# Adapter weights as the stationary operand of the setup's matmuls, and the first unit's step sizes on VectorE

## The chip, the cores and the metric

The kernel runs on one core of a Trainium2 chip. The core has five engines with queues of their own: TensorE (PE, with its weight loads listed apart as PEld), VectorE (DVE), ScalarE (ACT), GpSimd (POOL) and SyncE (SP), which here only issues DMAs. Each engine works its queue in the order of the program and waits on semaphores for the others. The metric is the device time of one execution in microseconds (us); less is better.

## What is computed

The reference runs four layers over x, 16 sequences of 256 steps and 256 features, all in float32, with a condition vector of 256 numbers for each sequence. Layer 0 makes adapter matrices from the condition and applies them:

```python
h = gelu(layernorm(ada_emb, ln_g, ln_b) @ W1 + b1)     # (16, 256)
w = h @ W2 + b2                                        # (16, 256 * 8 * 4)
a1, bb1, a2, bb2 = split(w, 4)                         # each (16, 256, 8): feature, rank
y = gelu((x @ a1) @ bb1.T)                             # per sequence
x = x + (y @ a2) @ bb2.T
```

Layer 1 is a selective state space model, forward and backward in time. Its step sizes are dt = softplus(xs @ xproj_w + bias); for each of 512 channels and 64 states the recurrence is h = h * exp(dt * A) + dt * xs * B, and the output sums h * C over the states. Layers 2 and 3 are attention and feed-forward blocks whose scales, shifts and gates are matmuls of the same condition ("modulation").

## The kernel before

**The loop.** There are 32 units: 16 sequences by two directions. For each unit the kernel takes 64 states one after another. GpSimd makes the products dt * xs * B (`drive`, L926), ScalarE the decays exp(dt * A) (`decay`, L941), VectorE scans over time (L969) and multiplies by C (L972; for three states of eight GpSimd does it, L976), and TensorE adds up over the states (L987). The next unit's front and the rest of a sequence's layers are interleaved by Python generators: `step(gen)` records the next piece of a generator, up to its next `yield`.

**The setup.** Ahead of the loop stands the setup, which this change is about.

- L169 to L191: SP issues the loads of the condition, of W1 (`w_ada`), of many small bias rows, and of the first tiles of W2. `load_w2(i)` loads the i-th of eight tiles of W2: 256 rows by 1024 columns in two halves `w` of 128 rows each, 512 KB. Columns are 128 features by 8 ranks with the rank running fastest. The halves take turns in the 11 buffers (`NH`) that later hold the loop's `h`. Three tiles are loaded up front (L194).
- L197 to L247: transposes, the layer norm and W1 give `hid`, the activated hidden layer, with features on the partitions: 2 halves of 128 x 16 sequences.
- L994 to L1037: the tile loop, which makes the four adapter matrices (`mats`: `lows[0]`, `turned[0]`, `lows[1]`, `turned[1]`, each of 2 halves of 128 features). For tile i, `hid` is the stationary operand (128 x 16) and the W2 tile streams past it, 512 columns at a time (L1005). The result has the 16 sequences on its partitions, so it is copied to SBUF (`wrow`, L1008, one half by VectorE and one by ScalarE), and one step later eight transposes of 16 x 128, one for each rank, turn it (L1020). VectorE adds the bias b2 (L1021). When both halves of a `turned` matrix are there, they are transposed once more (L1030) and written to scratch memory in DRAM (`spill`, L1035). The loop issues the load of tile i + 3, and at i = 2 that of the first sequence (`load_adapter(0)`) and of the first unit's projection weights (`load_front(0)`: `w_in`, `w_dt`). From i = 4 on it takes a step of the generator `modulation` (L215: 12 matmuls with 128 x 128 weights and 16 moving columns).
- L1038 `load_ups(0)`: the first sequence's rows of `spill` come back as `hi`.
- `front(0)` (L373): the adapter is applied (L341 `px` to L362), layer norm, input projection (L393, `w_in`), Silu (L399), the projections to B and C (L404) and to the step sizes (L423, `w_dt`). Softplus follows as max(p, 0) + log(1 + exp(-|p|)), with a correction for the rounding of 1 + exp(-|p|): ScalarE makes the pieces (L438 to L447) and GpSimd puts them together in four operations over 128 x 1024 elements (L452, L455, L458, and L461, which makes `dtx` = dt * xs, the input of every product in L926).
- Meanwhile the second unit's front and `late()` begin: `late()` makes the modulations of the later layers (L215 again, closed by L222 and L228 on VectorE), pads the weights of layer 3 (L1061 to L1086) and derives some biases (L1110).

**What sets the order.** Operations go to a scheduler, which may place them ahead of others in an engine's queue; those in `tc.keep_in_program_order` keep their place. Matmul results use PSUM tiles of 128 x 512 from a pool of two (`bank1`, `bank2`), so a third one waits until one of the two before it is read out. SP issues DMAs in the order of its queue: one that waits for a free buffer holds up those behind it.

Of the kernel before, what the change touches and what calls it, by code (L numbers as in the profile page):

```python
# [8 lines left out]
F32 = mybir.dt.float32  # L9
AF = mybir.ActivationFunctionType  # L10
ALU = mybir.AluOpType
# [4 lines left out]
P = 128  # L16
B, T, D = 16, 256, 256
DC = D // P
NT = T // P
RANK = 8  # L20
DI = 512
IC = DI // P
# [32 lines left out]
def kernel(ctx: ExitStack, tc: tile.TileContext, a: dict, out: bass.AP):  # L55
    nc = tc.nc
# [4 lines left out]
    ident = const.tile([P, P], F32, name="ident")  # L61
# [76 lines left out]
    def chunked(w):  # L138
        return w.rearrange("(c p) f -> p c f", p=P)

    def bank1(name="bank1"):
        return ps_g.tile([P, 512], F32, tag="bank2", name=name)
# [14 lines left out]
    def halves(t):  # L157
        return t.rearrange("p (c t) -> p c t", c=2)
# [6 lines left out]
    p2 = early.enter_context(tc.tile_pool(name="p2", bufs=2))  # L165
# [17 lines left out]
    b2 = p1.tile([P, 4, DC, RANK], F32, name="b2")  # L183
    nc.sync.dma_start(b2, a["L0_cond_b2"].rearrange("(m c p r) -> p m c r", m=4, c=DC, p=P))

    def load_w2(i):
        ws2 = []
        for k in range(DC):
            w = s3.tile([P, P * RANK], F32, tag="h", name="w2", bufs=NH)
            nc.sync.dma_start(w, a["L0_cond_W2"][k * P : (k + 1) * P, i * P * RANK : (i + 1) * P * RANK])  # L190
            ws2.append(w)  # L191
        return ws2

    w2s = [load_w2(i) for i in range(3)]  # L194

    pt = bank1("pt_rows")
    nc.tensor.transpose(pt[:, :P], rows, ident)  # L197
# [42 lines left out]
    hid = p1.tile([P, DC, B], F32, name="hid")  # L240
# [81 lines left out]
    def load_adapter(b):  # L322
        dtxs[2 * b] = s2.tile([P, IC, T], F32, name="dtx")
        xin = dtxs[2 * b][:, 0:2]
        nc.sync.dma_start(xin, a["x"][b].rearrange("(t p) d -> p t d", p=P))
        adapt[b] = xin
# [38 lines left out]
    def load_front(u):  # L365
        d = ("fwd", "bwd")[units[u][1]]
        wi = ws.tile([P, DC, 2 * DI], F32, tag="ws", name="w_in")
        nc.sync.dma_start(wi, chunked(a[f"L1_cond_{d}_in_w"]))
        wd = ws.tile([P, IC, DI], F32, tag="ws", name="w_dt")
        nc.sync.dma_start(wd, chunked(a[f"L1_cond_{d}_xproj_w"])[:, :, 0:DI])  # L370
        wfront[u] = (wi, wd)

    def front(u):  # L373

        b, d = units[u]
        name = ("fwd", "bwd")[d]
        if d == 0:
            yield from adapter(b)
            hT = s1.tile([P, DC, T], F32, name="hTm")
            sq = s1.tile([P, DC, T], F32, name="sqm", tag="uu")  # L380
            yield from layernorm(
                xs[b], hT, sq, bank1,
                lambda c: m_mamba[:, 2 + c, b : b + 1], lambda c: m_mamba[:, c, b : b + 1], T,
            )
            normed[b] = hT
        hT = normed[b]
        w_in, w_dt = wfront.pop(u)
        xz = s2.tile([P, 2 * IC, T], F32, name="xz")
        for m in range(0, 2 * IC, 2):
            px = halves(bank1("pxz"))  # L390
            for j in range(2):
                for c in range(DC):
                    nc.tensor.matmul(  # L393
                        px[:, j], w_in[:, c, (m + j) * P : (m + j + 1) * P], hT[:, c],
                        start=(c == 0), stop=(c == DC - 1),
                    )
                yield
            nc.scalar.copy(xz[:, m : m + 2], px)
        nc.scalar.activation(xz, xz, AF.Silu)  # L399
        exp_table()  # L400
        yield
        pb = bank1("pbc")
        for c in range(IC):
            nc.tensor.matmul(pb[:, :T], w_bc[d][:, c], xz[:, c], start=(c == 0), stop=(c == IC - 1))  # L404
        bc = s1.tile([P, T], F32, name="bc", tag="uu")
        nc.scalar.copy(bc, pb[:, :T])
        bd = bdram.tile([P, T], F32, name="bd")
        nc.sync.dma_start(bd, bc)
        yield
        pt = bank1("pct")  # L410
        for t in range(NT):
            nc.tensor.transpose(pt[:, t * P : (t + 1) * P], bc[:, t * P : (t + 1) * P], ident)
        cT = s2.tile([P, NT, NS], F32, name="cT")
        nc.scalar.copy(cT, pt[:, :T].rearrange("p (t s) -> p t s", t=NT)[:, :, NS:])
        yield


        pr = s1.tile([P, IC, T], F32, name="pr")
        for m in range(0, IC, 2):
            pp = halves(bank1("pdt"))  # L420
            for j in range(2):
                for c in range(IC):
                    nc.tensor.matmul(  # L423
                        pp[:, j], w_dt[:, c, (m + j) * P : (m + j + 1) * P], xz[:, c],
                        start=(c == 0), stop=(c == IC - 1),
                    )
                yield
            for j in range(2):
                nc.scalar.activation(  # L429
                    pr[:, m + j], pp[:, j], AF.Identity, bias=col(f"L1_cond_{name}_dt_bias", m + j)  # L430
                )
            yield
        if u + 1 < len(units):
            load_front(u + 1)
        if d == 1:
            dtxs[u] = s2.tile([P, IC, T], F32, name="dtx")
        dtx = e = dtxs.pop(u)
        nc.scalar.activation(e, pr, AF.Abs)  # L438
        yield
        nc.scalar.activation(e, e, AF.Exp, scale=-1.0)  # L440
        nc.scalar.activation(pr, pr, AF.Relu)
        yield
        dt = s2.tile([P, IC, T], F32, name="dt")
        uu = s1.tile([P, IC, T], F32, name="uu")
        nc.scalar.activation(uu, e, AF.Identity, bias=1.0)
        nc.scalar.activation(dt, uu, AF.Ln)
        nc.scalar.activation(uu, uu, AF.Identity, bias=minus)  # L447
        yield
        yield
        yield  # L450
        yield
        tc.keep_in_program_order(nc.gpsimd.tensor_tensor(uu, e, uu, ALU.subtract))  # L452
        yield
        yield
        tc.keep_in_program_order(nc.gpsimd.tensor_tensor(dt, dt, uu, ALU.add))  # L455
        yield
        yield
        tc.keep_in_program_order(nc.gpsimd.tensor_tensor(dt, dt, pr, ALU.add))  # L458
        yield
        yield  # L460
        tc.keep_in_program_order(nc.gpsimd.tensor_tensor(dtx, dt, xz[:, 0:IC], ALU.mult))  # L461
        st[u] = (xz, cT, bd, dt, dtx)
        yield

# [527 lines left out]

    turned = [p1.tile([P, DC, B, RANK], F32, name=f"up{k}") for k in range(2)]
    mats = [lows[0], turned[0], lows[1], turned[1]]
    wrows = {}
    for i in range(9):
        if i < 8:
            w2 = w2s[i]  # L1000
            wrow = p2.tile([B, P * RANK], F32, tag="wrow", name="wrow")
            for n in range(2):
                pw = bank1("pw")
                for k in range(DC):
                    nc.tensor.matmul(  # L1005
                        pw[:B], hid[:, k], w2[k][:, n * 512 : (n + 1) * 512], start=(k == 0), stop=(k == DC - 1)
                    )
                (nc.scalar.copy if n else nc.vector.tensor_copy)(wrow[:, n * 512 : (n + 1) * 512], pw[:B])  # L1008
            wrows[i] = wrow
            if i + 3 < 8:  # L1010
                w2s.append(load_w2(i + 3))
            if i == 2:
                load_adapter(0)
                load_front(0)
        if i > 0:
            m, c = (i - 1) // 2, (i - 1) % 2
            wv = wrows.pop(i - 1).rearrange("b (d r) -> b d r", r=RANK)
            pw = bank1("pwt")
            for r in range(RANK):
                nc.tensor.transpose(pw[:, r * B : (r + 1) * B], wv[:, :, r], ident[:B, :B])  # L1020
            nc.vector.tensor_tensor(  # L1021
                mats[m][:, c],
                pw[:, : RANK * B].rearrange("p (r b) -> p b r", b=B),
                b2[:, m, c, :].unsqueeze(1).to_broadcast([P, B, RANK]),
                ALU.add,
            )
            if m % 2 and c:
                ph = bank1("pmt")
                for c in range(DC):
                    nc.tensor.transpose(  # L1030
                        ph[:, c * P : (c + 1) * P], mats[m][:, c].rearrange("p b r -> p (b r)"), ident
                    )
                upT = p1.tile([P, D], F32, name=f"upT{m}")
                nc.scalar.copy(upT, ph[:, :D])
                nc.sync.dma_start(spill[:, m // 2], upT)  # L1035
        if i > 3:
            step(mamba)  # L1037
    load_ups(0)  # L1038
    drain(mamba)
# [99 lines left out]
    for k in range(len(steps) + BEHIND):  # L1139
        if k < len(steps):  # L1140
            u, s = steps[k]
# [11 lines left out]
        if k >= BEHIND:  # L1153
            u, s = steps[k - BEHIND]
            if s == NS - 1:
                b, d = units[u]
# [4 lines left out]
                for i in range(2):  # L1161
                    py = halves(bank1("py"))
                    for j in range(2):
                        c = 2 * i + j
# [45 lines left out]
```

## Time and profile before

| | |
|---|---|
| median of 3 runs | 7628.08 us (7628.05 to 7632.17) |
| the profiled execution | 7630.37 us, its span 7628.6 us |
| busy: TensorE, VectorE, ScalarE, GpSimd | 82%, 90%, 70%, 91% of the span |
| mean granted TensorE clock | 0.928 |
| tile loop: first matmul L1005 to last turn L1030 | 27.14 to 73.23 us |
| first product L926, first scan L969 | 135.09, 137.47 us |

The span runs from the first to the last recorded instruction. A share of busy time is a mean over stages that have different limits: setup, loop and tail are to be read apart. "Idle before" in a row names what ended an engine's wait. The granted clock is the share of its full clock that TensorE's throttle lets through.

### The profile page before, as it was taken

What the parts mean: (1) busy time and instruction counts of PE and PEld (TensorE: products, weight loads), DVE (VectorE), ACT (ScalarE), POOL (GpSimd) and SP (SyncE); (2) the same over time, 40 slices, a digit from 0 to 9 for tenths busy, and PEclk for the clock granted to TensorE, in tenths of its full rate; (3) what the DMA queues carried; (4) which work ended last, traced back from release to release, by engine and by line L of the source; (5) the groups of instructions that cost most, each with busy time, mean ns of one, the idle gap of its engine ahead of it and who ended that gap; (6) DMA issues with size and microseconds to landing.
All of it is one profiled execution on the core that took longest, in us unless ns stands there. A gap on an engine that the chain in (4) does not pass through costs nothing. (4 is left out here: it accounts for less than half of the span.)

```text
span 7628.6 us, 100211 instructions
## 1 busy us (share of the span) xinstructions
PE 6253.0 (82%) x35215; PEld 4947.6 (65%) x35215; DVE 6886.1 (90%) x6951; ACT 5370.7 (70%) x12013; POOL 6912.3 (91%) x2991
## 2 busy tenths in 40 slices
PE   6568888888888888888888888888888888888778
PEld 4456666666667666666666667666666666667655
DVE  3988998999999999999999999899999999999972
ACT  3567776777767777776777777777776777777653
POOL 3999999999999999999999999999999999999960
PEclk8679999999999999999999999999999999999999
DMA  4112232222322222232222222222232222222211
GB/s 167 52 60 93 85 103 73 92 90 87 108 79 96 79 95 94 92 103 73 85 100 86 100 86 97 78 92 93 87 105 78 92 85 96 94 92 92 72 64 49
DMA packets 331642, 675.87 MB, mean 89 GB/s; under 512 B 24724, under 2 KB 204032, under 8 KB 326784
## 3 DMA queue, kind: packets, MB, share of 16 engines
q1 hardware_dynamic: 331136, 669.44, 26.0%
q8 instruction: 278, 4.55, 0.2%
q14 instruction: 228, 1.87, 0.1%
HBM read 650.22 MB, written 10.75 MB: 87 GB/s over the span
## 5 line engine op out<-in xcount | busy, mean ns | idle before, releaser
L969 DVE TENSOR_TENSOR_SCAN h<-decay,h 128x512 f32<-128x512 f32 x4096 | 4735.2, 1204 | 271.5 <-ACT decay L941 189.3
L926 POOL TENSOR_TENSOR h<-dtx,bb 128x1024 f32<-128x1024 f32 x2048 | 4794.8, 2370 | 79.9 <-PE y L987 79.8
L987 PE MATMUL y<-ident,h 128*128 128x128 f32 x16384 | 2457.7, 296 | 836.8 <-POOL h L976 798.8
L987 PEld LDWEIGHTS y<-ident,h 128*128 128x128 f32 x16384 | 2083.4, 153 | 1216.4 <-POOL h L976 940.9
L941 ACT ACTIVATE decay<-dt,a_neg_bwd 128x255 f32<-128x255 f32 x4096 | 1814.5, 469 | 824.1 <-DVE h L969 777.0
L941 ACT ACTIVATE decay<-dt,a_neg_fwd 128x255 f32<-128x255 f32 x4096 | 1807.9, 471 | 641.1 <-DVE h L969 598.9
L976 POOL TENSOR_TENSOR h<-h,cb 128x1024 f32<-128x1024 f32 x768 | 1816.5, 2365 | 199.5 <-DVE h L969 172.0
L972 DVE TENSOR_TENSOR h<-h,cs 128x1024 f32<-128x1024 f32 x1280 | 1526.0, 1204 | 73.7 <-PE cs L956 62.9
L956 PE MATMUL cs<-ident,cT 128*128 128x128 f32 x2560 | 503.6, 290 | 88.5 <-DVE h L972 86.1
L956 PEld LDWEIGHTS cs<-ident,cT 128*128 128x128 f32 x2560 | 332.1, 146 | 163.4 <-DVE h L972 123.9
L573 PE MATMUL sc<-k,q 64*128 64x256 f32 x960 | 283.1, 417 | 17.7 <-ACT ex L582 17.0
L393 PE MATMUL pxz<-hTm,w_in 128*128 128x256 f32 x1024 | 275.8, 387 | 15.4 <-DVE maxima L683 12.3
L582 ACT ACTIVATE ex<-sc,nmax 128x256 f32<-128x256 f32 x480 | 222.1, 468 | 71.9 <-DVE nmax L578 69.1
L701 PE MATMUL scT<-qk,kd 128*128 128x256 f32 x984 | 248.8, 385 | 28.6 <-DVE qk L692 23.1
L680 PE MATMUL sc<-kd,qk 128*128 128x512 f32 x490 | 252.0, 621 | 14.2 <-DVE maxima L683 10.0
L596 ACT COPY exT<-pt 128x512 f32<-128x512 f32 x240 | 139.8, 583 | 162.7 <-PE pt L592 162.4
L423 PE MATMUL pdt<-xz,w_dt 128*128 128x256 f32 x1024 | 245.9, 383 | 0.0
L573 PEld LDWEIGHTS sc<-k,q 64*128 64x128 f32 x960 | 167.0, 193 | 99.8 <-ACT ex L582 32.9
L701 PEld LDWEIGHTS scT<-qk,kd 128*128 128x128 f32 x984 | 176.1, 190 | 58.3 <-ACT pr L429 24.9
L393 PEld LDWEIGHTS pxz<-hTm,w_in 128*128 128x128 f32 x1024 | 179.2, 193 | 43.2 <-DVE maxima L683 15.7
L423 PEld LDWEIGHTS pdt<-xz,w_dt 128*128 128x128 f32 x1024 | 189.4, 193 | 21.8
L578 DVE TENSOR_REDUCE nmax<-sc 128x2 f32<-128x512 f32 x240 | 162.1, 676 | 35.7 <-PE sc L573 35.5
(348 smaller groups left out, 7530.1 us busy)
## 6 DMA issues: line engine op xcount, KB each, us to landing
bb<-bd SPq DMA_DIRECT2D x512, 512.0 KB
cb<-bd SPq DMA_DIRECT2D x256, 384.0 KB
l2w<-in_L_cond_W_dram SPq DMA_DIRECT2D x32, 1024.0 KB
l3w<-in_L_cond_W_dram SPq DMA_DIRECT2D x32, 1024.0 KB
l1w<-in_L_cond_mlp_w_dram SPq DMA_DIRECT2D x48, 512.0 KB
w_in<-in_L_cond_fwd_in_w_dram SPq DMA_DIRECT2D x16, 1024.0 KB
w_dt<-_L_cond_fwd_xproj_w_dram SPq DMA_DIRECT2D x16, 1024.0 KB
w_in<-in_L_cond_bwd_in_w_dram SPq DMA_DIRECT2D x16, 1024.0 KB
```

What stands on the lines that cost most here:

```text
L393: nc.tensor.matmul(px[:, j], w_in[:, c, (m + j) * P : (m + j + 1) * P], hT[:, c], start=(c == 0), stop=(c == DC - 1),)
L423: nc.tensor.matmul(pp[:, j], w_dt[:, c, (m + j) * P : (m + j + 1) * P], xz[:, c], start=(c == 0), stop=(c == IC - 1),)
L573: nc.tensor.matmul(sc[:, t], q[base : base + 64, ch, t * P : (t + 1) * P], k[base : base + 64, ch], start=True, stop=True,)
L680: nc.tensor.matmul(sc, q[:, g, t * P : (t + 1) * P], kd[g % 2][:, 2 * i : 2 * i + 2], start=True, stop=True)
L701: nc.tensor.matmul(sc[:, kt], kd[g % 2][:, j, kt * P : (kt + 1) * P], q[:, g], start=True, stop=True)
L926: nc.gpsimd.tensor_tensor(h, st[u][4], bb.unsqueeze(1).to_broadcast([P, IC, T]), ALU.mult)
L941: nc.scalar.activation(dc[:, j, 1:T], st[u][3][:, c, when], AF.Exp, scale=a_neg[d][:, c, s : s + 1])
L956: nc.tensor.transpose(cs[:, i % 2, t * P : (t + 1) * P], st[u][1][:, t, s : s + 1].to_broadcast([P, P]), ident)
L969: nc.vector.tensor_tensor_scan(hv, dv, hv, 0.0, ALU.mult, ALU.add)
L972: nc.vector.tensor_tensor(h, h, c.unsqueeze(1).to_broadcast([P, IC, T]), ALU.mult)
L976: nc.gpsimd.tensor_tensor(h, h, c.unsqueeze(1).to_broadcast([P, IC, T]), ALU.mult)
L987: nc.tensor.matmul(ys[u][:, t, c * P : (c + 1) * P], h[:, c, t * P : (t + 1) * P], ident, start=(s == 0 and c == 0), stop=(s == NS - 1 and ...
```

## The change

In the tile loop the operands change places. For each rank the 128 features of a W2 half are the stationary operand, every eighth of its columns (`w2[k][:, :, r]`), and `hid` (16 columns) moves; two halves add up in PSUM, and the result has the features on its partitions at once. The `wrow` copies and the transposes L1020 go, and the bias is added straight from the matmul's PSUM tile. A tile has 16 matmuls of 16 moving columns where it had 4 of 512 and 8 transposes. Five tiles are loaded up front instead of three, and the modulation's steps begin one tile earlier in the count (`i > 2`). Lastly, the four step size operations go to VectorE for unit 0 alone.

```diff
-    w2s = [load_w2(i) for i in range(3)]
+    w2s = [load_w2(i) for i in range(5)]
...
+        pool = nc.gpsimd if u else nc.vector
...
-        tc.keep_in_program_order(nc.gpsimd.tensor_tensor(uu, e, uu, ALU.subtract))
+        tc.keep_in_program_order(pool.tensor_tensor(uu, e, uu, ALU.subtract))
...
-        tc.keep_in_program_order(nc.gpsimd.tensor_tensor(dt, dt, uu, ALU.add))
+        tc.keep_in_program_order(pool.tensor_tensor(dt, dt, uu, ALU.add))
...
-        tc.keep_in_program_order(nc.gpsimd.tensor_tensor(dt, dt, pr, ALU.add))
+        tc.keep_in_program_order(pool.tensor_tensor(dt, dt, pr, ALU.add))
...
-        tc.keep_in_program_order(nc.gpsimd.tensor_tensor(dtx, dt, xz[:, 0:IC], ALU.mult))
+        tc.keep_in_program_order(pool.tensor_tensor(dtx, dt, xz[:, 0:IC], ALU.mult))
...
-    for i in range(9):
-        if i < 8:
-            w2 = w2s[i]
-            wrow = p2.tile([B, P * RANK], F32, tag="wrow", name="wrow")
-            for n in range(2):
-                pw = bank1("pw")
-                for k in range(DC):
-                    nc.tensor.matmul(
-                        pw[:B], hid[:, k], w2[k][:, n * 512 : (n + 1) * 512], start=(k == 0), stop=(k == DC - 1)
-                    )
-                (nc.scalar.copy if n else nc.vector.tensor_copy)(wrow[:, n * 512 : (n + 1) * 512], pw[:B])
...
-            for r in range(RANK):
-                nc.tensor.transpose(pw[:, r * B : (r + 1) * B], wv[:, :, r], ident[:B, :B])
...
+    for i in range(8):
+        w2 = [w.rearrange("p (d r) -> p d r", r=RANK) for w in w2s[i]]
+        m, c = i // 2, i % 2
+        pw = bank1("pw")
+        for r in range(RANK):
+            for k in range(DC):
+                nc.tensor.matmul(
+                    pw[:, r * B : (r + 1) * B], w2[k][:, :, r], hid[:, k], start=(k == 0), stop=(k == DC - 1)
+                )
...
+        if i + 5 < 8:
+            w2s.append(load_w2(i + 5))
...
-        if i > 3:
+        if i > 2:
             step(mamba)
```

More of the change, by code (lines that the diff above doesn't have):

```diff
@@ L996 @@
     mats = [lows[0], turned[0], lows[1], turned[1]]
-    wrows = {}
-    for i in range(9):
-        if i < 8:
-            w2 = w2s[i]
-            wrow = p2.tile([B, P * RANK], F32, tag="wrow", name="wrow")
-            for n in range(2):
-                pw = bank1("pw")
-                for k in range(DC):
-                    nc.tensor.matmul(
-                        pw[:B], hid[:, k], w2[k][:, n * 512 : (n + 1) * 512], start=(k == 0), stop=(k == DC - 1)
-                    )
-                (nc.scalar.copy if n else nc.vector.tensor_copy)(wrow[:, n * 512 : (n + 1) * 512], pw[:B])
[L1009 to L1018, printed above, removed]
-            for r in range(RANK):
[L1020 to L1026, printed above, removed]
+    for i in range(8):
[7 more added lines that the diff above has]
+                )
+        nc.vector.tensor_tensor(
+            mats[m][:, c],
+            pw[:, : RANK * B].rearrange("p (r b) -> p b r", b=B),
+            b2[:, m, c, :].unsqueeze(1).to_broadcast([P, B, RANK]),
+            ALU.add,
+        )
+        if i + 5 < 8:
+            w2s.append(load_w2(i + 5))
+        if i == 2:
+            load_adapter(0)
+            load_front(0)
+        if i >= 0:
             if m % 2 and c:
```

## The prediction, made before the changed kernel was timed

> **What bounds the kernel now.** I read the page's 40 slices first, then busy time and clock in short stretches of the first 140 us, then the timeline of that stretch, since the diff touches nothing later. Columns of the slices: one digit for each 190 us.
>
> ```profile
> DVE  3988998999999999999999999899999999999972
> POOL 3999999999999999999999999999999999999960
> PEclk8679999999999999999999999999999999999999
> ```
>
> From the second slice on VectorE and GpSimd are both over 80% busy: the unit loop (scan L969, products L926 and L976) sets the pace until the tail. The first slice is different (3 and 3): it holds a setup of 135 us in which one chain after another must end before the loop can start. I set the instruction orders of the two programs side by side: apart from names they differ only ahead of the first scan, on all five engine queues. So the change is worth what it does to the loop's start; nothing later can win it back or add to it except by chance of alignment. In the timeline (start, duration, engine, line, what; in brackets the idle time before and its releaser):
>
> ```profile
> 42.59 3.61 PE L1005 MATMUL pw<-w,hid 128*16 128x512 f32 x8 [0.38 <-DVE low L1021]
> ...
> 46.13 1.05 PE L1020 MATMUL pwt<-ident,wrow 16*128 16x16 f32 x8
> ...
> 47.21 0.29 DVE L1021 TENSOR_TENSOR up<-pwt,b 128x128 f32<-128x128 f32 x1 [1.96 <-PE pwt L1020]
> ...
> 52.80 2.90 PE L215 MATMUL pmod<-condT,wmod 128*128 128x16 f32 x24
> ...
> 73.07 0.60 PE L341 MATMUL px<-ident,dtx 128*128 128x128 f32 x4
> ```
>
> One adapter tile takes 4.97 us (37.62, 42.59, 47.55, 52.52 are the starts of four). TensorE works nearly all of it. The eight tiles with the modulation (L215) fill 27.14 to 73.07 us, and TensorE is the bound there: the DMA share falls to 0.24 in 45 to 50 us and to 0 in 65 to 70.
>
> **Part 1, the tile loop.** Removed per tile: 8 records of 512 moving columns (L1005), 8 transposes, two copies of 0.68 (VectorE) and 0.57 us (ScalarE). Added: 16 matmuls, 32 records (L215 shows two records for each fp32 matmul: 12 give 24), each with 128 x 128 weights and 16 moving columns. This is the shape of L215 and L244, so the nearest rows are good, but they come at two rates:
>
> ```profile
> 25.27 1.89 PE L244 MATMUL ph<-aT,w_ada 128*128 128x16 f32 x8 [3.82 <-ACT aT L117]
> ...
> 118.55 2.75 PE L215 MATMUL pmod<-condT,wmod 128*128 128x16 f32 x24
> ```
>
> L215: less one record's 0.26, 2.49 over 23 steps is 0.108 us each. L244: (1.89 - 0.37)/7 = 0.217; L1095, 8 in 1.85, gives 0.211. I take 0.213. A tile is 32 x 0.108 = 3.5 us at the one rate, 32 x 0.213 = 6.8 at the other, against 4.97 now. The sign of the change hangs on the clock. In stretches of half a microsecond (TensorE busy, records, granted clock, DMA share, GB/s):
>
> ```profile
> 53.50:54.00 0.50, 0.50 (x7) 1.00 0.00 0
> ...
> 55.00:55.50 0.50, 0.50 (x5) 0.75 0.68 123
> 55.50:56.00 0.50, 0.50 (x2) 0.50 0.84 264
> ...
> 58.50:59.00 0.50, 0.50 (x2) 0.84 0.92 313
> ```
>
> The clock halves at 55.25 (0.75 is half the stretch), **in the middle of L215's back-to-back run**, and comes back at 58.66, 3.41 later, after 512-column work. It halves again at 133.76 (0.88 in 133 to 134), 23 steps of 3.41 later; the first rise, seen in L1005's records going from 0.85 to 0.43 apart at 31.4, fits the same grid. (The clock column reads 1.00 before that, but the durations say half.) The stretch judged before 55.25 is 51.84 to 55.25: TensorE idles 0.4 of it, yet it counts as idle. The one before 133.76 had 2.5 us of L215. Between 116.7 and 130.3, where each such stretch also holds 1.8 to 2.6 us of 256-column work (L393), the clock stays. So what counts is moving columns: 16 take 13 ns (512 take 0.427 us) of a 108 ns record, 12%. In the new loop every record is such a one, and it starts at half clock.
>
> The Trainium skill (TensorE: Matmul & The Clock Gate, "Why this matters for your kernels") tells us to keep TensorE busy 4 us without a break to get the full clock. By that rule a loop of 32 back-to-back records warms up after one tile, and the page's weight load ("LDWEIGHTS", columns over 1.2 GHz, 107 ns for 128) makes a tile 3.4 us: the loop would end near 62. By the rows it stays at half clock. I take the rows: this trace has a run that was busy and lost the clock.
>
> The strided weights (every 8th element) cost nothing extra by the nearest row: L1020's weights have that stride, 8 loads in 0.95, (0.95 - 0.20)/7 = 0.107 each. That row has 16 partitions, not 128; below is no gain, above a doubling (+27 us warm, more cold). I take none.
>
> New end of the loop: start 27.14; 0.4 until the second half of hid is there; 8 x 6.83 = 54.6; L215's 24 records 5.1; tile 3's turn for the spill waits 0.7 for VectorE (L1021's 0.29 and two handovers) and takes 0.5; the last one 0.5 + 0.7 + 0.25. Sum 89.9, less 0.3 where a half turn overlaps tile 7: 89.6, against 73.07. **+16.5.**
>
> Five tiles ahead: 6 tile loads now stand in front of wmod and the small weights on SP, and the input, w_in and w_dt stand behind the last tile, whose buffer (11 for 16 loads) comes free when tile 2 is done, 48 us instead of 32.4. All land by 60 and are wanted from 89 on: nothing. TensorE waited for a tile 0.3 us in all: the earlier loads win nothing.
>
> **Part 2, what stands behind the loop.** The clock is now half in px, pl and phigh too. Until phigh the spill's way round (L1035, then hi, phigh at 77.44, 4.4 after px) hides it: px and pl cold make 4.1. SP issues wmod (768 KB, some 2 us at the 400 GB/s of 25 to 45 us) between spill and hi, where it now issues it long before: 0 to +2, I take +0.5, as hi also no longer stands behind wvp, which waited for a memset until 75.01. phigh then takes 2.07 (its second run) for 1.10: +1.0. L393 got its clock 3.7 after its start; on a 3.41 grid this is 3.4 to 6.8, half the excess is lost: +0.7. The w3pad copies wait for w3raw, now loaded behind the last spill, near 100; ScalarE has 5.8 us free there (low at 81.19+0.36, sqm at 87.37) for 2.0 us of copies: nothing. **+2.2.**
>
> **Part 3, the first unit's step sizes.**
>
> ```profile
> 125.39 2.35 POOL L452 TENSOR_TENSOR uu<-dtx,uu 128x1024 f32<-128x1024 f32 x1 [36.94 <-PE pxz L393]
> ...
> 127.98 0.26 DVE L222 TENSOR_TENSOR m_l<-pmod,colb 128x96 f32<-128x96 f32 x1 [6.18 <-PE pmod L215]
> ...
> 132.91 0.26 DVE L222 TENSOR_TENSOR m_l<-pmod,colb 128x96 f32<-128x96 f32 x1 [2.61 <-PE pmod L215]
> ...
> 135.09 13.90 POOL L926 TENSOR_TENSOR h<-dtx,bb 128x1024 f32<-128x1024 f32 x6
> ...
> 137.47 2.34 DVE L969 TENSOR_TENSOR_SCAN h<-decay,h 128x512 f32<-128x512 f32 x2 [2.32 <-POOL h L926]
> ```
>
> Four operations of 2.35 to 2.43 a step leave GpSimd; on VectorE the nearest row is L972, the same size, 1.20. Alone this would save 4.6. But in VectorE's order uu stands behind the first L222 and the third operation behind the second, and both wait for L215 on TensorE. In the old times: uu 128.25, the small m_l and gb operations 0.36, second operation until 131.0; L222 at 132.91 to 133.17; third until 134.4; 0.36; dtx until 136.0, against 135.0 on GpSimd. **+1.0.** GpSimd's first product, then the scan, follow at once. The decays need dt (134.4) and start at 135.45, behind ScalarE's Silu. The Trainium skill (SBUF — State Buffer, "Who interferes with whom") says that a VectorE operation with two SBUF inputs shuts out a GpSimd one that reads SBUF: a rule against this edit. But the rows show GpSimd with nothing to run ahead of dtx (idle 36.94 before L452), so it costs nothing here; with work beside it, up to 2.4 an operation. The two 1.9 us stalls of L228 beside GpSimd go, off the path.
>
> **Sum:** 16.5 + 2.2 + 1.0 = +19.7. The profiled execution took 7630.37 (span 7628.6 and 1.8 around it), so 7650; the median of the three runs is 2.3 lower, so **7648** is forecast.
>
> **Rivals.** *The clock comes up in the tile loop* (the other side, 0.12): for it, the skill's rule, and that neither idle stretch was filled to the end with such work. Against: 2.45 of 3.41 us were. Price: 32 x 0.105 = 3.4 us a tile. With all eight warm after 3.4 us cold, the loop ends at 89.6 - 27 - 2.5 + 2 = 62; with parts 2 and 3 at +2, about 7619. It is as fast as before from six warm tiles on; from two on it can't be told from no change. *The lock stalls in the first unit fall otherwise* (0.08): an L228 at 180.70 took 12.25 us, because GpSimd ran without a gap, and GpSimd then idled 9.5. If a shift makes or spares one such stall, -10 or +10: 7638 or 7658. Against: scan and products start in the same order from the same event. *Strided weights at half rate* (0.03): 7700. *The edit's aim holds, VectorE's order doesn't hurt* (0.05): -5, 7643.
>
> **How the numbers follow.** The case of half clock has 0.72, 7641 to 7656 by the bounds of hi (-0.5 to +1.5), grid (-1 to +3) and record step (0.211 to 0.217: -0.5 to +1.2), and some for alignment. For 8 in 10 the range goes from 7634, which takes in a partly warm loop and a spared stall, to 7660. 0.2% is 15.3 us, about what a measurement tells from no change: over 7643.4 lie 0.62 of the 0.72, half of the stalls, the strided case and some of the last one: 0.72 slower. Faster needs 7612.8, below even the warm loop: 0.02. The rest, 0.26, is the same.
>
> **What would show it.** Right: the records of the new matmuls 0.21 apart to the end, px near 89.6, granted clock 0.5 until L393; dtx waiting on VectorE behind L222; first scan near 157. Wrong: a clock of 1.00 in the tile loop with records 0.11 apart, px before 75; steps other than these two (strides); or a scan start as forecast and an end that moved by another amount.

## The result, and the profile after

| | before | changed |
|---|---|---|
| median of 9 runs each | 7628.57 us | 7650.76 us |
| lowest, highest | 7625.46, 7635.22 | 7647.19, 7652.98 |
| ratio, 95% interval | | 1.0026, 1.0018 to 1.0035 |
| profiled execution, its span | 7630.37, 7628.6 us | 7651.89, 7650.1 us |

The changed kernel is slower by 22.2 us by the medians (0.29%; the ratio says 0.26%); 19.7 us were forecast. Beyond the first slices its page looks like the one before. Line numbers of the changed kernel differ: L1008 is now the bias (L1021 before), L1023 the last turn (L1030), and the loop's lines are one higher.

```profile
DVE  2989999999999999999999999999999999999972
POOL 1999999999999999999999999999999999999960
PEclk9678999999999999999999999999999999999999
```

The loss is in the first digit: VectorE 2 for 3, GpSimd 1 for 3. The unit loop starts later. The timeline of the tile loop (start, duration, engine, line, what):

```profile
27.50 30.62 PE L1005 MATMUL pw<-hid,w 128*128 128x16 f32 x128
...
42.94 0.29 DVE L1008 TENSOR_TENSOR low<-pw,b 128x128 f32<-128x128 f32 x1 [7.32 <-PE pw L1005]
50.55 0.29 DVE L1008 TENSOR_TENSOR up<-pw,b 128x128 f32<-128x128 f32 x1 [7.32 <-PE pw L1005]
...
60.34 7.75 PE L1005 MATMUL pw<-hid,w 128*128 128x16 f32 x32
67.92 3.57 PE L215 MATMUL pmod<-condT,wmod 128*128 128x16 f32 x16
...
95.13 1.06 PE L341 MATMUL px<-ident,dtx 128*128 128x128 f32 x4
```

A tile's bias comes 7.61 us after the one before it (42.94, 50.55). TensorE never pauses in the loop, so its 32 records are 7.61/32 = 0.238 apart. Between tiles the modulation L215 goes at (3.57 - 0.37)/15 = 0.213, the half-clock rate of the prediction. So px starts at 95.13 instead of 73.07. (The clock column reads 1.00 here until 131 us, and the page's first PEclk digit is even 9 for 8. The column shows changes only and no starting state; the durations of L215 and of px, 1.06 for 0.60, say half.)

The first unit's step sizes on VectorE:

```profile
152.56 0.26 DVE L222 TENSOR_TENSOR m_l<-pmod,colb 128x96 f32<-128x96 f32 x1 [6.18 <-PE pmod L215]
152.74 1.23 DVE L453 TENSOR_TENSOR uu<-dtx,uu 128x1024 f32<-128x1024 f32 x1
...
157.49 0.26 DVE L222 TENSOR_TENSOR m_l<-pmod,colb 128x96 f32<-128x96 f32 x1 [2.20 <-PE pmod L215]
157.66 1.22 DVE L459 TENSOR_TENSOR dt<-dt,pr 128x1024 f32<-128x1024 f32 x1
...
162.72 2.34 DVE L970 TENSOR_TENSOR_SCAN h<-decay,h 128x512 f32<-128x512 f32 x2 [2.52 <-POOL h L927]
```

As forecast, uu and the third operation each start right behind an L222 that waited for TensorE (6.18 and 2.20 us). The first scan is at 162.72, 25.25 later than before; the end is only 21.5 later. In the first unit 6.6 us come back: from the first product to the second unit's uu it takes 97.13 us (160.34 to 257.47) for 103.70 before. Behind it 2.8 are lost again; where was not traced, and single executions of one kernel differ by more (7625.46 to 7635.22).

### The profile page after: what moved, and what is told of

It is laid out like the page before. It is cut to its first block, busy times and chain, and to the rows that moved or that the text cites. A ratio compares the mean times of both kernels' runs of the same rounds, so it can differ in the third digit from the quotient of the medians.

```text
span 7650.1 us, 100438 instructions
## 1 busy us (share of the span) xinstructions
PE 6282.4 (82%) x35343; PEld 4991.5 (65%) x35343; DVE 6877.5 (90%) x6947; ACT 5384.5 (70%) x12005; POOL 6904.7 (90%) x2987
## 5 line engine op out<-in xcount | busy, mean ns | idle before, releaser
L393 PE MATMUL pxz<-hTm,w_in 128*128 128x256 f32 x1024 | 277.1, 389 | 15.4 <-DVE maxima L684 12.4
L393 PEld LDWEIGHTS pxz<-hTm,w_in 128*128 128x128 f32 x1024 | 179.8, 194 | 43.5 <-DVE maxima L684 15.7
```

The source lines that it names most:

```text
L393: nc.tensor.matmul(px[:, j], w_in[:, c, (m + j) * P : (m + j + 1) * P], hT[:, c], start=(c == 0), stop=(c == DC - 1),)
```

## The experiments

All were seen in a trace; those with an interval were timed in rounds beside the kernel before. Runs made together share a chip, and the median of before lay between 7621.82 and 7628.57 from chip to chip, so single times are not set against each other here: starts and steps within the traces are.

**Adjacent columns as weights.** It tells half clock from stride. The adapter matrices then hold other columns.

```diff
-  pw[:, r * B : (r + 1) * B], w2[k][:, :, r], hid[:, k], ...
+  pw[:, r * B : (r + 1) * B], w2s[i][k][:, r * P : (r + 1) * P], hid[:, k], ...
```

> The changed kernel with 128 adjacent columns of W2 as the weights of each matmul instead of every eighth (the adapter matrices then hold other columns than they should). Measured in the changed kernel: 0.238 us from record to record in the tile loop, tiles 7.61 us apart, px at 95.1 us. Theory (half clock, since 16 moving columns hardly count as work; the stride is a small extra): 0.213 a record as in L215 at half clock, a tile 6.8 us, px near 89, the whole 6 us shorter. Rival 1 (the stride is the cause, and TensorE has its full clock as the clock column says): 0.107 a record, a tile 3.4 us, px near 62, the whole 33 us shorter. Rival 2 (a fixed price of a weight load and matmul pair): 0.238, nothing moves.

The timeline of this run, one tile and the modulation behind it:

```profile
57.45 6.99 PE L1005 MATMUL pw<-hid,w 128*128 128x16 f32 x32
64.27 3.57 PE L215 MATMUL pmod<-condT,wmod 128*128 128x16 f32 x16
...
89.23 1.06 PE L341 MATMUL px<-ident,dtx 128*128 128x128 f32 x4
```

(6.99 - 0.37)/31 = 0.2135 a record, and px at 89.23: 5.9 us earlier than in the changed kernel, near the 89.6 of the prediction. Without the stride the loop runs as forecast, at half clock, and is still 16 us late. Both rivals fall as the sole cause. But at half clock the stride adds (0.238 - 0.2135) x 256 = 6.3 us.

**The clock held up.** Matmuls with 512 moving columns that compute nothing, into `cs`, which is free during the setup; tiles 4 to 7 with adjacent columns (and so other values).

```diff
+    wide(8)
     for i in range(8):
...
+                wk = w2[k][:, :, r] if i < 4 else w2s[i][k][:, r * P : (r + 1) * P]
...
+            if r % 4 == 3:
+                wide(2)
```

> The changed kernel with matmuls of 512 moving columns that compute nothing: eight ahead of the tile loop, two after every four ranks of a tile (half of TensorE's time). Tiles 0 to 3 take every eighth column as weights as before, tiles 4 to 7 adjacent columns (so the second adapter pair holds other columns). Theory (clock): the wide matmuls bring the clock up, after that the small records are 0.107 apart in tiles 4 to 7 and 0.12 to 0.13 in tiles 0 to 3; a tile with its four wide matmuls takes 32 x 0.12 + 3.4 = 7.2 us, about what it took without them, and px at half clock behind the loop is not needed: it starts warm. Rival 1 (stride): 0.238 in tiles 0 to 3 and 0.107 in tiles 4 to 7. Rival 2 (fixed price of a pair): 0.238 in all eight.

Its timeline, small records (L1016) and wide ones (L1004):

```profile
36.42 3.98 PE L1016 MATMUL pw<-hid,w 128*128 128x16 f32 x16
40.32 2.51 PE L1004 MATMUL cs<-wide_src,hid 128*16 128x512 f32 x4
42.76 3.98 PE L1016 MATMUL pw<-hid,w 128*128 128x16 f32 x16
...
72.05 3.99 PE L1016 MATMUL pw<-hid,w 128*128 128x16 f32 x16
...
108.15 1.89 PE L1004 MATMUL cs<-wide_src,hid 128*16 128x512 f32 x4
109.97 1.96 PE L1016 MATMUL pw<-hid,w 128*128 128x16 f32 x16
```

And its granted clock (stretch, TensorE busy and records, clock, DMA share, GB/s):

```profile
41.00:42.00 1.00, 1.00 (x3) 0.73 0.00 0
...
44.00:45.00 1.00, 1.00 (x6) 0.50 0.00 0
...
74.00:75.00 1.00, 1.00 (x6) 1.00 0.00 0
...
110.00:111.00 1.00, 1.00 (x11) 1.00 0.00 0
```

No theory got this whole. Adjacent columns at full clock: (1.96 - 0.26)/15 = 0.113, as the clock theory says. Every eighth column: (3.98 - 0.40)/15 = 0.24 at 42.76, with the clock at 0.50, and as much, (3.99 - 0.40)/15, at 72.05, with the clock at 1.00 (72.2 to 75.6). Full clock makes them no faster; the clock theory forecast 0.12 to 0.13.

In tiles 0 to 3 the wide matmuls did not hold the clock: it went at 41.46 (0.73 is the mean of 41 to 42) and came back five times, each time for one stretch of 3.41 us. In tiles 4 to 7 it stayed, from 106.3 to 137.0.

So there are two limits: at half clock the small records take 0.213, and strided weights take 0.24 at either clock. Each alone would make a tile slower than the 4.97 us before (6.8 and 7.6). In the changed kernel the second one sets the pace: its loop would take 0.238 a record at full clock too.

**Which strides.** Tiles with different weights, wide matmuls between every eight small records; the matrices hold nothing useful.

```diff
+        s, q = ((1, P), (2, P), (4, P), (8, P), (8, 64), (8, 16), (0, P), (1, 16))[i]
...
+                    wk = w2s[i][k][:q].rearrange("p (d r) -> p d r", r=s)[:, 0:P, r % s]
+                    nc.tensor.matmul(dst, wk, hid[:q, k], start=(k == 0), stop=(k == DC - 1))
+                else:
+                    nc.tensor.transpose(cs[:, 0, :P], w2[k][:, :, r], ident)
+            if r % 2 == 1:
+                wide(3)
```

In the expectation, read the list that closes its first sentence ("step 1, 2, 4, 8 ..."); what stands just before that list is a slip.

> A measurement, not a version: after 16 wide matmuls that bring the clock up, each of the eight tiles runs its 16 small matmuls with other weights, six wide ones among every eight records (so the clock should stay up): tile 0 adjacent columns, 1 every second, 2 every fourth, 3 every eighth, 4 every eighth with 64 rows, 5 eighteenth-free transposes of every eighth column of 128 rows, 6 is left to the next line; in the order of the tiles: step 1, 2, 4, 8 with 128 rows, step 8 with 64 rows, step 8 with 16 rows, transposes of step 8 with 128 rows, step 1 with 16 rows (the adapter matrices hold nothing useful). In the run with wide matmuls, step 8 took 0.24 a record at a granted clock of 1.00, and adjacent columns 0.113. Theory A (the load of weights reads a fixed number of bytes at a time, so a wider step costs more reads): 0.11 for step 1, more for 2 or 4, 0.24 for 8, the same for all numbers of rows. Theory B (any step but 1 falls to one slow rate): 0.24 for 2, 4 and 8 alike. Theory C (the price depends on the rows too, which would explain why the 16-row transposes of the kernel before showed 0.107): 0.24 with 128 rows, less with 64, 0.107 with 16. Theory D (transposes are exempt): 0.107 in the tile of transposes.

The timeline, one group each of step 1, 2, 4 and 8 with 128 rows, step 8 with 16 rows, and transposes of step 8:

```profile
44.16 1.06 PE L1019 MATMUL pw<-hid,w 128*128 128x16 f32 x8
...
58.85 1.11 PE L1019 MATMUL pw<-hid,w 128*128 128x16 f32 x8
...
73.75 2.04 PE L1019 MATMUL pw<-hid,w 128*128 128x16 f32 x8
...
92.34 2.08 PE L1019 MATMUL pw<-hid,w 128*128 128x16 f32 x8
...
138.70 2.07 PE L1019 MATMUL pw<-hid,w 16*128 16x16 f32 x8
...
152.73 0.71 PE L1021 MATMUL cs<-ident,w 128*128 128x128 f32 x4
```

Less the last record's own time (0.26 and 0.27 in the first two groups, 0.38 and 0.39 in the next two), over 7: 0.114, 0.12, 0.237 and 0.241 us. The price doubles between a step of two and of four float32 elements; the clock stood at 1.00 but for the stretch behind the modulation. Rows don't matter (16 rows as 128; 64 rows took 2.07 too), so theory C falls. Neither A nor B describes it quite: no steady rise, but one step; why it sits there no run shows. The transposes come out at (0.71 - 0.27)/3 = 0.15; of the three steps in the group the first is 0.215, the other two are 0.111. So theory D holds but for a group's first step, and the row on which the prediction rested, L1020, was misleading because it holds transposes and not because it has 16 rows.

**The step sizes back on GpSimd**, in the changed kernel:

```diff
-        pool = nc.gpsimd if u else nc.vector
+        pool = nc.gpsimd
```

> The changed kernel with the first unit's four step size operations back on GpSimd. From the first modulation's L222 (m_mlp) to the first scan: 16.14 us before, 16.82 in the changed kernel. Theory (VectorE's order holds these operations behind two waits for TensorE): 16.1, the scan starts 0.7 us earlier. Rival (VectorE's shorter operations win, and the 0.7 comes from the clock or the loads of this stretch): 17.5 or more. The end of the kernel may move by more, as the first unit's lock stalls can fall otherwise: no forecast of it.

m_mlp's L222 is at 145.85 and the first scan at 161.99: 16.14, as before. The 0.7 us is the edit's own.

**Three tiles ahead**, in the changed kernel:

```diff
-    w2s = [load_w2(i) for i in range(5)]
+    w2s = [load_w2(i) for i in range(3)]
...
-        if i + 5 < 8:
-            w2s.append(load_w2(i + 5))
+        if i + 3 < 8:
+            w2s.append(load_w2(i + 3))
```

> The changed kernel with three tiles loaded up front instead of five. Theory (TensorE is the bound of the tile loop, the loads are early either way): px within 0.5 us of the changed kernel's 95.1. Rival (the earlier loads feed the loop): px 2 us or more later, TensorE waiting for tiles by DMA.

px at 95.05, 67.8 after the loop's first record (67.6 in the changed kernel). The earlier loads do nothing.

**The step sizes alone** on VectorE, in the kernel before:

> The kernel before with nothing but the first unit's four step size operations on VectorE. Theory: from the first modulation's L222 (m_mlp) to the first scan 16.8 us, where the kernel before has 16.1; the whole within 0.2% of before. Rival (the operations save what they are shorter): 14 or less.

121.89 to 138.70: 16.81, as forecast, and the rival falls. This run took 7617.5 and its first unit was shorter, so the same kernel was timed:

> The same kernel as in the run of the step size operations alone (before, with the four operations of the first unit on VectorE), now timed. In the one look its first scan came 16.8 us after m_mlp as forecast, 0.7 later than before, but from the first product to the second unit's uu it took 97.2 us, where before takes 103.7, and the whole was 7617.5. Theory: the lock stalls of the first unit fall otherwise and give back 4 to 7 us; the whole 0.1% faster, ratio 0.9985 to 1.0000. Rival (chance of one run): ratio 1.000 to 1.001, and the stretch near 103 again.

0.9993, interval 0.9985 to 1.0001 (7620.27 to 7627.80 by the medians): not told from no change. But the stretch in question repeated: from the first product to the second unit's uu 97.1 us, where the kernel before has 103.7. VectorE's waits beside GpSimd, the prediction's "lock stalls", show it; first the kernel before, then this one, then the run with adjacent columns:

```profile
180.70 12.25 DVE L228 TENSOR_SCALAR m_l<-m_l 128x32 f32<-128x32 f32 x1
```

```profile
183.03 1.78 DVE L228 TENSOR_SCALAR m_l<-m_l 128x32 f32<-128x32 f32 x1
...
187.15 2.28 DVE L228 TENSOR_SCALAR m_l<-m_l 128x32 f32<-128x32 f32 x1
```

```profile
202.62 11.04 DVE L228 TENSOR_SCALAR m_l<-m_l 128x32 f32<-128x32 f32 x1
```

An operation that takes 0.18 alone took 12.25, until GpSimd's products paused at 192.91. In the timed kernel two of them take some 2 us each, though GpSimd works without a pause there too (177.76 to 194.00). With VectorE's step sizes the stretch took 96.7 to 99.2 us in six kernels of this study (the changed one 97.1), but 104.1 with adjacent columns; with GpSimd's it took 99.8 to 104.1 in four. So the edit that costs 0.7 us in front mostly spares several behind, but not always.

The long wait tells the runs apart better than the edit does. All four runs above 100 us have one (11.04 to 12.25); the eight below have none, and one of these is the changed kernel with its step sizes back on GpSimd (1.77 and 2.29; 99.8 us). What decides whether the wait occurs was not settled.

**A version from what the runs point to.** The operands of the kernel before (wide moving data, which holds the clock), but `hid` padded to 32 columns, so that four column groups of TensorE each take two ranks; five tiles ahead, step sizes on GpSimd.

```diff
+            for k in range(DC):
+                for j in range(4):
+                    nc.tensor.matmul(
+                        pw[32 * j : 32 * j + 32, : 2 * P],
+                        hid4[:, k],
+                        w2[k].rearrange("p (d r) -> p d r", r=RANK)[:, :, 2 * j : 2 * j + 2],
+                        start=(k == 0), stop=(k == DC - 1),
+                    )
+            nc.vector.tensor_copy(wrow, pw[:, : 2 * P])
...
+            for r in range(2):
+                nc.tensor.transpose(pw[:, r * P : (r + 1) * P], wv[:, :, r], ident)
```

> The kernel before with its operands (hid is the weights, W2 moves), but hid padded to 32 columns and four column groups of TensorE working on two ranks each: a tile is 8 matmuls of 256 columns, one copy, and 2 transposes of 128 x 128 in place of 4 of 512 columns, 2 copies and 8 small transposes; five tiles ahead; step sizes on GpSimd. If the four groups run side by side the 16 records of a tile take about 0.9 us, TensorE is no longer the bound, and px starts when the last tile of W2 is in, near 48 to 52 (73.07 before): 20 us shorter than before, 7608. If they run one after the other a tile takes 3.4 + 0.5 us: px near 64, 9 us shorter, 7619. If the clock theory holds the moving columns keep the clock up in both cases; if only the rate of pairs counts, 24 records a tile at 0.238 give 5.7 us and no gain.

```profile
31.70 1.12 PE L1008 MATMUL pw<-w,hid 128*32 128x256 f32 x16
32.76 0.51 PE L1026 MATMUL pwt<-ident,wrow 128*128 128x128 f32 x2
33.38 1.12 PE L1008 MATMUL pw<-w,hid 128*32 128x256 f32 x16
```

A tile's 16 records take 1.12 us: the four groups run side by side (an estimate for one after the other, at half of the 0.43 us that 512 columns take: 3.4). Tiles are 1.68 apart, px is at 46.46 and the first scan at 113.59, 23.9 earlier than before. 7600.11 us, ratio 0.9965 (0.9952 to 0.9979): faster than the kernel before, and so than the changed one. The clock stood at 1.00 from 31.7 to 52.2, beyond px, and then at 0.50 to 72.7. What the tiles loaded ahead give here was not separated.

Two additions to it. With wide matmuls in TensorE's gaps behind px:

> The version with four column groups, and wide matmuls that compute nothing in TensorE's gaps from px to the end of the first Silu, to hold the clock up there (in the version without them pl, phigh and the two layer norm sums took 1.9 to 2.07 each, and the input projection L393 9.3). Theory (wide work holds the clock): granted clock 1.00 from px on, those five at about 1.1, L393 7.1, first scan 4 to 7 us earlier than 113.6, the whole about 0.4% faster than before. Rival (the wide matmuls stand in the way as much as they win): first scan within 2 us of 113.6.

From px to 103.5 the clock was 1.00 but for some 3.4 us near 63 to 66, and the input projection took 7.17 for 9.32. But the first product came only 0.3 us earlier (110.87 for 111.20), since `low` now stood on ScalarE behind a `w3pad` copy that waited for its load (TensorE idled 3.41). Then the clock fell to 0.50 until 117.1: the last modulation in front of the scan took 5.14 for 2.75, VectorE's m_l operations waited for it and stood ahead of the scan, and the first scan came at 115.59, 2.0 later than without. The ratio is 0.9965 (0.9953 to 0.9977), nothing won: the rival was right.

With the step sizes on VectorE:

> The version with four column groups, and the first unit's four step size operations on VectorE. If what these give back in the first unit holds here too, the stretch from the first product to the second unit's uu is 97 to 99 us (104.1 without) and the ratio to before 0.9955 to 0.9965; if not, 104 and 0.9965 to 0.9970.

The stretch took 97.1, and the ratio was 0.9965 (0.9952 to 0.9977): the first half of the expectation held, the time doesn't tell.

## Why the prediction was right, and where not

- *The loop's start decides:* right. Of the 25.25 us at the first scan, 22.06 arise before px.
- *Half clock in the tile loop:* right as to the clock (L215 between the tiles at 0.213, adjacent columns at 0.2135 to the end), and with the clock alone px is 16 us late. But in this loop the clock is not what sets the pace: the stride gives 0.238 at full clock too. That the sum for half clock came near is in part luck. (The stretches of 3.41 us from 116.7 to 130.3, given as holding 1.8 to 2.6 us of L393, hold 1.85 to 1.99; the argument stands.)
- *"The strided weights cost nothing extra by the nearest row":* wrong, the term that was mis-sized. Set at 0, it measured +6.3 here: 0.238 a record instead of 0.213, a tile 7.61 instead of 6.83. The rival "half rate" (given 0.03) names the right effect: at full clock the stride doubles a record. Its price of +27 us, "more cold", was too high, because a strided record takes no longer at half clock. The start was 0.4 later than before (27.50), turns and modulation about 1 less than summed, so px came at 95.13 and not 89.6.
- *The rival that the clock comes up:* the rule cited for it, 4 us of unbroken work, did not hold here: TensorE worked from 27.50 to 94.47 without a pause, and px at 95.13 still took 1.06 us. The rival's price was wrong too. It set 3.4 us a tile at full clock; measured with this stride, 32 x 0.24 = 7.7. Clock or no clock, this loop could not have reached the 4.97 of the kernel before. That half clock came to nearly the same figure hid the second limit.
- *Part 2:* from px to m_mlp's L222 it took 50.77 for 48.26, +2.5 for +2.2. The wait for hi was 1.3 longer (0.5 taken, up to 1.5 allowed), the rest less.
- *Part 3:* +0.7 for +1.0, by the mechanism named.
- *Nothing behind the first scan:* wrong in size. The case "lock stalls fall otherwise" (given 0.08) came true beside the main one and gave back 6.6 us by the second unit; 3.75 are left at the end. That offset most of what the stride added.

In sum 22.06 + 2.5 + 0.7 - 3.75 = 21.5 of span, 22.2 by the medians. The total was met more closely than its terms: +5.5 in the loop stood against -3.75 behind, and that is luck. Of the prediction's own signs, records 0.21 apart, px near 89.6 and a first scan near 157 did not come (0.238, 95.13, 162.72); the half clock and dtx waiting behind L222 did.

## What to carry to other kernels

Before data and weights change places on TensorE, count moving columns per record: with 16 of them behind 128 columns of weights the engine was busy without a break and lost its clock before, or never got it in the changed kernel. Take the price of a strided weight load from a matmul with that stride, not from a transpose. If few rows are wanted (16 sequences here), keep the wide operand moving and give each column group of TensorE its own part: that took a tile from 4.97 to 1.68 us and kept the clock through the loop.

## What the runs showed that was not expected

- A matmul record whose float32 weights have a step of four or more elements takes twice as long at full clock (0.24 for 0.113 us), with 16 rows as with 128; a step of two is nearly free (0.12), and transposes of step 8 take 0.111 after the first. At half clock the same stride costs 11% (0.238 for 0.2135): the strided record takes the same time at either clock.
- Wide matmuls in half of the time held the clock up beside adjacent columns (1.82 of 3.71 us), and beside step 8 when they were more (2.68 of 4.68 us in the run with strides). When 1.14 of the 3.41 us before 41.46 were wide, it went.
- A VectorE operation of 0.18 us can take 12.25 beside a row of GpSimd operations without a pause (176.67 to 192.91), and some 2 us beside another such row (177.76 to 194.00 in the timed kernel with the step sizes on VectorE).
